# A correlation gram in two half-width blocks of 64 tokens, placed beside attention, in a two-layer f32 kernel

## The chip, the cores and the metric

The kernel runs on one core of a Trainium2 chip. The metric is device microseconds of one execution; of several runs the median counts. The profile is one further execution, recorded by the hardware profiler.

## What is computed

Eight images of 768 channels and 32 x 32 pixels (1024 tokens) pass two layers, each a residual around a group norm.

```python
# layer 0: attention whose scores come from variances
qkv = gn(x).reshape(8, 768, 1024).swapaxes(1, 2) @ W_qkv.T       # 12 heads of 64
scores = var(v) @ var(k).T * scale                               # outer product of two vectors
x = x + proj(softmax(scores) @ v)
# layer 1: 1x1 convolution over 768 channels and 28 correlation channels
f = gn(x)
n = f / max(norm(f over channels), 1e-12)
corr[r, c] = sum over channels of n shifted by (r - 3, c - 3), times n      # zero outside the image
x = x + conv_w @ concat(f, corr at 28 offsets of a 7 x 7 window) + conv_b
```

The 28 offsets are the two diagonals, the middle column and the middle row of the 7 x 7 window. Because a product of two tokens is the same seen from either, the kernel needs only the offsets that look ahead: 12 of them, at most 3 rows down and 3 columns to either side, and the token's product with itself for the norm. The other half is the same numbers shifted.

## The kernel before

Everything is f32. Products of keys and values, of the projection and of the convolution go through a seven-product scheme on blocks (`PAIR`, `SINGLE`, `ORDER`), with `L355` issuing nearly all of them: 128 x 384 moving columns for keys and values, 128 x 512 for projection and convolution. Attention computes, per pair of heads, exponentials on ScalarE (`ex`, L709), and multiplies them with the values on TensorE (`av`, L734): 64 columns for each of two heads, side by side in the array's columns. A run of attention is `STEPS` = 4 key tiles. For some pairs ScalarE also sums the denominators (`junk`, L719), for others VectorE adds the exponentials (`acc`) and TensorE sums them over partitions (`den`). `spread` takes variances on VectorE (`hdk`, `hdv`, `vm`), and `to_rows` transposes them on TensorE (`ptv`, `ptk`, L526) and sends them to DRAM, from where `Pair.rows` broadcasts them (`bc`, `bk`).

Images overlap: while attention of image b runs, the second half of its keys and values and layer 1 of image b - 1 are laid between the runs. The order of all engines' instructions is written by a planner at build time. A `Clock` counts planned microseconds; `later.after` puts a job at a planned time; `work_off` (L1229) takes attention runs whenever they can go, and otherwise the next unit of the list `rest`. Keys-and-values units are planned at `KV_US` = 1.94 us, convolution units at `T_US` = 2.6 us. If only `TAIL` = 14 us of `rest` are left, it waits for attention. Each engine then works strictly in this order. All DMAs but a few at the start go through SP's queue.

The correlation of an image (`Corr`) works on 8 blocks of 128 tokens, 4 rows of the image each. `gram` (L1046) multiplies a block's 128 tokens with the 227 tokens that start with it (`WIN` = 128 + 99), in 6 products over the channels: 128 columns of weights, 227 columns streamed. The last block has 128. The result is copied from PSUM by VectorE (`win`) and written to DRAM (`windowed`, L1056). `diagonals` (L1068) reads from there, with a row pitch one longer than the row, the 19 numbers of each token. `scale` makes the norms (`m`, `rn` on POOL at L1081, `dn`) with a `mask` for the left and right border, transposes (`ct`, L1092) and writes rows; `gather` shifts them and makes the channels `cs`, which the convolution's last products add (L976). The grams are units of 2.35 planned us inside `rest`, in the eighth image one after another behind the first two convolution units.

PSUM tiles of grams and transposes come from `other`, two buffers. POOL makes the sums for keys and values (`make_sums`, L572 to L578). `Conv.start` loads the residual x1 again (`x<-x1d`, L1144) into the buffer of the image whose keys and values are done; VectorE's first take of the convolution needs it. `Norm.apply` writes `f` on VectorE in six pieces.

Of the kernel before, what the change touches and what calls it, by code (L numbers as in the profile page):

```python
# [6 lines left out]
F32 = mybir.dt.float32  # L7
# [20 lines left out]
RUNS = ((0, 0, 4), (31, -1, 3), (62, -2, 5), (93, -3, 7))  # L28
AHEAD_OF = [o for first, _, count in RUNS for o in range(first, first + count)][1:]
NA = len(AHEAD_OF)  # L30
PAD = 99
WIN = P + PAD
# [16 lines left out]
KV_US, T_US, CORR_US = 1.94, 2.6, 1.05  # L49

# [102 lines left out]
def two_layers(ctx, tc, x, wkv, wproj, bproj, wconv, wcorr, bconv, out):  # L153
# [11 lines left out]
    winpool = pool("winpool", 2)  # L165
# [6 lines left out]
    junkpool = pool("junkpool", 1)  # L172
# [230 lines left out]
    windowed = [dconst.tile([MT, P, WIN], F32, name=f"windowed{i}") for i in range(2)]  # L403

    def mask_rows():
        nc.gpsimd.memset(mask, 1.0)
        for q in range(0, P, W):
            at = 0
            for _, right, count in RUNS:
                run = mask[q : q + W, at : at + count]  # L410
                for base, sign in ((right, 1), (W - 1 - right, -1)):
                    nc.gpsimd.affine_select(
                        out=run, in_=run, compare_op=ALU.is_ge, fill=0.0, base=base,
                        pattern=[[sign, count]], channel_multiplier=sign,
                    )
                at += count
# [262 lines left out]
    class Pair:  # L679
# [33 lines left out]
        def denominators(self, t, e):  # L713
# [4 lines left out]
            junk = junkpool.tile([P, N], mybir.dt.bfloat16, tag="junk", name=f"junk{self.b}_{self.hp}_{e}_{t}")  # L718
# [318 lines left out]
    class Corr:  # L1037
        def __init__(self, b, f):
            self.b, self.f = b, f

        def gram(self, t):
            b, f = self.b, self.f
            n = min(WIN, N - t * P)
            ps = other([P, WIN], f"gr{b}_{t}")
            for j in range(J):
                nc.tensor.matmul(  # L1046
                    ps[:, :n], lhsT=f[:, j, t * P : (t + 1) * P], rhs=f[:, j, t * P : t * P + n],
                    start=j == 0, stop=j == J - 1,
                )

            def out():
                win = winpool.tile([P, WIN], F32, tag="win", name=f"win{b}_{t}")
                if n < WIN:
                    vector.memset(win[:, n:WIN], 0.0)
                vector.tensor_copy(win[:, :n], ps[:, :n])
                nc.sync.dma_start(out=windowed[b % 2][t], in_=win)  # L1056
                if t % 4 == 3:
                    later.after(4.0, lambda: self.diagonals(t // 4))

            later.after(2.6, out)  # L1060

        def diagonals(self, hf):
# [4 lines left out]
            for first, _, count in RUNS:  # L1067
                nc.sync.dma_start(  # L1068
                    out=dd[:, :, at : at + count],
                    in_=windows(windowed[b % 2][4 * hf, 0:1, first:], (WIN + 1, P), (P * WIN, 4), (1, count)),  # L1070
                )
                at += count
            later.after(6.0, lambda: self.scale(hf, dd))

        def scale(self, hf, dd):
# [14 lines left out]
            def to_dram(dn):  # L1090
# [3 lines left out]
                vector.tensor_copy(cr, pt[0 : 4 * NROW, 0:P])  # L1094
# [134 lines left out]
    def work_off(rest, attention=None):  # L1229
        while rest or (attention and not attention.over()):  # L1230
            if attention and not attention.over():
                clock.feed_act()
                if attention.can_run():
                    attention.run()
                    continue
# [116 lines left out]
    second = []  # L1352
# [5 lines left out]
    for b in range(NB + 1):  # L1358
        rest, attention, ots = [], None, None
# [5 lines left out]
        if b:  # L1365
# [4 lines left out]
            corr = Corr(b - 1, f)  # L1370
# [3 lines left out]
            grams = [(2.35 if t < MT - 1 else 1.45, has_f, lambda t=t: corr.gram(t)) for t in range(MT)]  # L1374
            first, start = (0.0, has_f, conv.sums.first), (0.0, (), conv.start)
            if b < NB:
                for n, gram in enumerate(grams):
                    rest.insert(2 * (n + 1) + n if b > 1 else 10 + 2 * n, gram)
# [13 lines left out]
        work_off(rest, attention)  # L1392
        if b < NB:
# [4 lines left out]
            elif b + 1 < NB:  # L1398
                clock.wait(("xn", b + 1), ready=ready)
                kv = KeysValues(b + 1, images[b + 1])  # L1400
                work_off(kv.units(0))
# [38 lines left out]
```

## Time and profile before

| | |
|---|---|
| Median of 3 runs | 2721.05 us (2720.9 to 2723.45) |
| Span of the profiled execution | 2722.5 us |
| Its distance from the median | 1.45 us above |
| Granted TensorE clock, mean | 0.998 |
| POOL, `make_sums` (L572 to L578) | 256 operations of 128 x 384, 1.0 to 1.08 us mean |
| VectorE, copy of a gram (`win`) | 64, 0.39 us |
| SP, window writes to DRAM | 64 of 113.5 KB, 0.32 us to issue |
| DMA, all | 448.9 MB, 165 GB/s |

The span is the time from the core's first instruction to its last. A row of a group of instructions gives line, engine, operation, tiles and shape, then how many, the time in which at least one of them ran, the mean length of one, and the idle time of the engine ahead of them. An f32 product appears as two instructions, each with a weight load of its own. [...] what a matmul costs the stream is the distance from its start to the next start.

### The profile page before, as it was taken

To read this page: it belongs to the slowest core of one execution; us is meant where nothing else is said; L and a number is where in the kernel's file an instruction comes from. 1 tells how busy PE (TensorE), PEld (TensorE's weight loads), DVE (VectorE), ACT (ScalarE), POOL (GpSimd) and SP (SyncE) were. 2 spreads that over 40 slices of the span, in tenths; PEclk is the share of its full clock that TensorE was granted. 3 is DMA by queue.
4 is the path that set the end of the run, shared out by engine and by line. 5 is a ranking of instruction groups with operands and counts; after the bars stand their busy time and mean duration, and the time that the engine had idled before them with its cause. 6 is when DMAs were issued, how large, how long until landed. Compare 5 with 4: busy or idle time off the path is not lost.

```text
span 2722.5 us, 28868 instructions
## 1 busy us (share of the span) xinstructions
PE 2685.7 (99%) x9063; PEld 1272.9 (47%) x9063; DVE 1666.8 (61%) x4168; ACT 1362.4 (50%) x1825; POOL 308.0 (11%) x350
## 2 busy tenths in 40 slices
PE   7999999999999999999999999999999999999999
PEld 4443454345543455434654346543465334653354
DVE  5859735785357853588535874357743577436863
ACT  1397078610797008960188601895019850198500
POOL 4320100003100031001210012100121001210000
PEclk9999999999999999999999999999999999999999
DMA  7864455464553655636556365463654526545233
GB/s 275 297 230 137 142 194 146 147 205 147 161 179 112 210 157 160 189 97 206 166 156 185 89 212 174 142 187 92 230 171 137 179 85 233 180 120 162 88 115 101
DMA packets 323603, 448.90 MB, mean 165 GB/s; under 512 B 59714, under 2 KB 245426, under 8 KB 323450
## 3 DMA queue, kind: packets, MB, share of 16 engines
q1 hardware_dynamic: 322218, 444.29, 51.7%
q10 hardware_dynamic: 1232, 2.75, 0.3%
q8 instruction: 73, 1.20, 0.2%
q14 instruction: 80, 0.66, 0.1%
HBM read 377.49 MB, written 67.38 MB: 163 GB/s over the span
## 4 chain that ended last, share of the span: by engine, by line
PE 87%; issue 6%; DVE 4%; DMA 2%; POOL 0%; SPq 0%; ACT 0%; DVEq 0%; POOLq 0%; ACTq 0%
PE x L355 33%; PE av L734 21%; PE y L355 17%; PE z L355 9%; PE gr L1046 3%; DMA x<-x1d 1%; PE den L767 1%; DVE dn L147 1%; PE x L976 1%; PE den L817 1%; DVE t2f L147 1%; PE y L976 1%; PE z L976 1%; DVE cs L147 0%; DMA ws<-in_wkv_dram 0%
## 5 line engine op out<-in xcount | busy, mean ns | idle before, releaser
L709 ACT ACTIVATE ex<-bc,nk 128x1024 f32<-128x1024 f32 x768 | 828.6, 1137 | 501.2 <-DMA bc<-vdr 309.3
L734 PE MATMUL av<-ex,v 128*64 128x512 f32 x3072 | 691.9, 597 | 0.9 <-ACT ex L709 0.8
L719 ACT ACTIVATE junk<-bk,vm 128x1024 bf16<-128x1024 f32 x368 | 420.4, 1142 | 20.0 <-DMA bk<-kdr 13.9
L734 PEld LDWEIGHTS av<-ex,v 128*64 128x64 f32 x3072 | 217.5, 137 | 445.5 <-issue 401.5
L147 DVE TENSOR_TENSOR acc<-acc,ex 128x1024 f32<-128x1024 f32 x350 | 401.9, 1216 | 0.0
L210 ACT COPY kp<-x 128x384 f32<-128x384 f32 x28 | 13.4, 478 | 557.0 <-PE x L355 557.0
L355 PE MATMUL x<-kv,xn 128*128 128x384 f32 x756 | 261.6, 493 | 2.8 <-DMA ws<-in_wkv_dram 1.6
L355 PE MATMUL y<-kv,s 128*128 128x384 f32 x744 | 258.8, 488 | 0.0
L355 PE MATMUL x<-kv,s 128*128 128x384 f32 x744 | 254.3, 488 | 0.0
L355 PEld LDWEIGHTS x<-kv,xn 128*128 128x128 f32 x756 | 142.8, 192 | 113.2 <-issue 17.1
L355 PEld LDWEIGHTS x<-kv,s 128*128 128x128 f32 x744 | 139.3, 190 | 103.4 <-issue 14.1
L355 PEld LDWEIGHTS y<-kv,s 128*128 128x128 f32 x744 | 138.2, 190 | 92.8 <-issue 5.6
L1046 PE MATMUL gr<-f 128*128 128x227 f32 (+1 forms) x672 | 131.4, 345 | 0.0
L355 PE MATMUL x<-v,wt 128*128 128x512 f32 x288 | 130.2, 596 | 0.0
L1046 PEld LDWEIGHTS gr<-f 128*128 128x128 f32 x672 | 121.6, 190 | 16.5 <-issue 3.0
L355 PE MATMUL z<-kv,xn 128*128 128x384 f32 x372 | 126.2, 487 | 0.0
L147 DVE TENSOR_TENSOR v<-y,v 128x128 f32<-128x128 f32 x180 | 41.0, 283 | 122.9 <-PE y L355 122.8
L355 PE MATMUL x<-f,wt 128*128 128x512 f32 x252 | 115.3, 598 | 0.0
L468 POOL TENSOR_TENSOR rstda<-vea,neghalf 128x1 f32<-128x1 f32 x8 | 4.8, 595 | 913.7 <-DVE vea L147 913.7
L147 DVE BATCH_NORM_STATS2 vbn<-v 128x6 f32<-128x64 f32 x720 | 101.9, 213 | 0.0
L572 POOL TENSOR_TENSOR s<-xn 128x384 f32<-128x384 f32 x64 | 68.5, 1080 | 291.7 <-PE x L355 204.7
L355 PEld LDWEIGHTS z<-kv,xn 128*128 128x128 f32 x372 | 70.0, 190 | 48.9 <-issue 3.8
(188 smaller groups left out, 2921.4 us busy)
## 6 DMA issues: line engine op xcount, KB each, us to landing
kv<-kvs SPq DMA_DIRECT2D x124, 576.0 KB
kv<-in_wkv_dram SPq DMA_DIRECT2D x95, 576.0 KB
bc<-vdr SPq DMA_DIRECT2D x96, 512.0 KB
f<-in_x_dram SPq DMA_DIRECT2D x48, 512.0 KB
bk<-kdr SPq DMA_DIRECT2D x46, 512.0 KB
x1d<-f SPq DMA_DIRECT2D x42, 512.0 KB
x<-x1d SPq DMA_DIRECT2D x42, 512.0 KB
out_dram<-x SPq DMA_DIRECT2D x82, 256.0 KB
```

What stands on the lines that cost most here:

```text
L147: return getattr(self.engine, name)(*args, **kw)
L210: nc.scalar.copy(to, at)
L355: nc.tensor.matmul(t, lhsT=lhsT, rhs=rhs, start=p in FIRST and k == 0, stop=stop and k == len(pairs) - 1, skip_group_check=True,)
L468: nc.gpsimd.tensor_tensor(self.rstd, ve, neghalf[:, 0:1], ALU.pow)
L572: nc.gpsimd.tensor_tensor(self.sums[g][:, 0], a[g][2], a[g][3], ALU.add)
L709: nc.scalar.activation(ex, self.bc[e], AF.Exp, scale=self.kv.nk[self.half][:, h, t : t + 1])
L719: nc.scalar.activation(junk, self.bk[e], AF.Exp, scale=self.kv.m2[self.half][:, h, t : t + 1], accum_out=self.sums[:, e, t : t + 1],)
L734: nc.tensor.matmul(self.av[e * HD : (e + 1) * HD, hf, :], lhsT=self.vt[:, t, e, :], rhs=exs[e][:, hf * HF : (hf + 1) * HF], start=t == 0, ...
L767: nc.tensor.matmul(den[at * 32 : (at + 1) * 32, :], lhsT=ones[:, 0:32], rhs=self.acc[e][:, hf * HF : (hf + 1) * HF], start=True, stop=True,)
L817: nc.tensor.matmul(den[e * HD : (e + 1) * HD, :], lhsT=ones, rhs=self.acc[e][:, at], start=True, stop=True)
L976: nc.tensor.matmul(t, lhsT=wcorr_sb[at, i, :], rhs=cs[at, tokens, :], start=False, stop=True, skip_group_check=True)
L1046: nc.tensor.matmul(ps[:, :n], lhsT=f[:, j, t * P : (t + 1) * P], rhs=f[:, j, t * P : t * P + n], start=j == 0, stop=j == J - 1,)
```

## The change

The gram of a block of 4 rows x 32 columns is computed as two blocks of 4 rows x 16 columns (64 tokens), one in each half of the array's columns. Each half streams its own moving operand: 7 rows of the image (`TALL`) by 19 columns (`WIDE`, 16 and 3 more), 133 columns in 7 pieces; 4 rows, 76 columns, for the last block. A weights operand in contiguous order is made first: `turn` copies the block, half by half, with POOL, into one buffer (`turnpool`); for the last image with ScalarE into the buffers of the exponentials, two blocks ahead. The window in DRAM gets another pitch, so that the diagonal read stays one step a token, and is written by two DMAs a gram of 4 x 16 rows of 136 numbers. `mask` follows the new order of tokens and is made of fewer POOL operations and eight small DMAs; the transposed rows are put back in image order by the copy `cr`.

The grams leave `rest` and stand in a list `beside`: `work_off` takes one ahead of and one behind each attention run, with two more given places among the first keys-and-values units from the third loop on (`next_to`), and the remainder ahead of the last units (`remaining`). Each is planned at `GRAM_US` = 1.45 us. `start_corr` makes an image's first turned block during the keys and values of the next image. The scratch output of the denominators shares a buffer with `ds` (`denpool`).

```diff
--- before.py
+++ after.py
@@ -26,10 +26,14 @@
 
 STEP = (33, 32, 31, 1)
 RUNS = ((0, 0, 4), (31, -1, 3), (62, -2, 5), (93, -3, 7))
+HW = W // 2
+TALL, WIDE = MT // 2 + 3, HW + 3
 AHEAD_OF = [o for first, _, count in RUNS for o in range(first, first + count)][1:]
 NA = len(AHEAD_OF)
 PAD = 99
-WIN = P + PAD
+SPAN = TALL * WIDE
+WIN = SPAN + 3
+PITCH = WIN + 3
 ROW = PAD + N + PAD
 NCORR = 28
 NCH = 2 * NA + 4
@@ -47,6 +51,7 @@
 TAIL = 14.0
 EXP, SUM, STEP_US = 1.07, 1.15, 1.77
 KV_US, T_US, CORR_US = 1.94, 2.6, 1.05
+GRAM_US = 1.45
 
 
 
@@ -162,14 +167,13 @@
     vopool = pool("vopool", HP)
     rdpool = pool("rdpool", 1)
     denpool = pool("denpool", 1)
-    winpool = pool("winpool", 2)
     kvpool = pool("kvpool", KVBLOCKS)
     wtpool = pool("wtpool", TBLOCKS)
     sumpool = pool("sumpool", 3)
     bcpool = pool("bcpool", 4)
     bkpool = pool("bkpool", 2)
     expool = pool("expool", 2 * AHEAD)
-    junkpool = pool("junkpool", 1)
+    turnpool = pool("turnpool", 1)
     wk = pool("wk", 3)
     uvpool = pool("uvpool", 1)
     st = pool("st", 1)
@@ -400,20 +404,28 @@
 
 
     rows = [dconst.tile([NROW, ROW], F32, name=f"rows{i}") for i in range(2)]
-    windowed = [dconst.tile([MT, P, WIN], F32, name=f"windowed{i}") for i in range(2)]
+    windowed = [dconst.tile([MT, P * (PITCH + 2)], F32, name=f"windowed{i}") for i in range(2)]
+    wins = [const.tile([P, WIN], F32, name=f"win{i}") for i in range(3)]
+    for win in wins:
+        nc.gpsimd.memset(win, 0.0)
+    across = const.tile([W, NA], F32, name="across")
 
     def mask_rows():
         nc.gpsimd.memset(mask, 1.0)
-        for q in range(0, P, W):
-            at = 0
-            for _, right, count in RUNS:
-                run = mask[q : q + W, at : at + count]
-                for base, sign in ((right, 1), (W - 1 - right, -1)):
-                    nc.gpsimd.affine_select(
-                        out=run, in_=run, compare_op=ALU.is_ge, fill=0.0, base=base,
-                        pattern=[[sign, count]], channel_multiplier=sign,
-                    )
-                at += count
+        nc.gpsimd.memset(across, 1.0)
+        at = 0
+        for _, right, count in RUNS:
+            run = across[:, at : at + count] if at else across[:, 0 : count - 1]
+            right, count = (right, count) if at else (1, count - 1)
+            for base, sign in ((right, 1), (W - 1 - right, -1)):
+                nc.gpsimd.affine_select(
+                    out=run, in_=run, compare_op=ALU.is_ge, fill=0.0, base=base,
+                    pattern=[[sign, count]], channel_multiplier=sign,
+                )
+            at += count
+        for q in range(P // HW):
+            side = q // (P // W)
+            nc.sync.dma_start(out=mask[q * HW : (q + 1) * HW, 1:], in_=across[side * HW : (side + 1) * HW, :])
 
     def load_corr_weights():
 
@@ -715,7 +727,7 @@
             if t == 0 and e == 0:
                 self.sums = st.tile([P, 2, MT], F32, tag="sums", bufs=2, name=f"sums{self.b}_{self.hp}")
             h = self.heads()[e][1]
-            junk = junkpool.tile([P, N], mybir.dt.bfloat16, tag="junk", name=f"junk{self.b}_{self.hp}_{e}_{t}")
+            junk = denpool.tile([P, N], mybir.dt.bfloat16, tag="den", name=f"junk{self.b}_{self.hp}_{e}_{t}")
             nc.scalar.activation(
                 junk, self.bk[e], AF.Exp, scale=self.kv.m2[self.half][:, h, t : t + 1],
                 accum_out=self.sums[:, e, t : t + 1],
@@ -1036,38 +1048,70 @@
 
     class Corr:
         def __init__(self, b, f):
-            self.b, self.f = b, f
+            self.b, self.f, self.turned = b, f, {}
+
+        def turn(self, t):
+
+            last = self.b == NB - 1
+            pl, tag = (expool, "ex") if last else (turnpool, "turn")
+            flat = pl.tile([P, N if last else J * P], F32, tag=tag, name=f"turn{self.b}_{t}")[:, : J * P]
+            self.turned[t] = flat.rearrange("p (j s m) -> p j s m", j=J, s=2)
+            to = flat.rearrange("p (j s y x) -> p j s y x", j=J, s=2, x=HW)
+            rows = self.f[:, :, t * P : (t + 1) * P].rearrange("p j (y s x) -> p j y s x", y=4, s=2)
+            for side in range(2):
+                if last:
+                    act_copy(0.5, to[:, :, side], rows[:, :, :, side, :])
+                else:
+                    nc.gpsimd.tensor_copy(to[:, :, side], rows[:, :, :, side, :])
 
         def gram(self, t):
-            b, f = self.b, self.f
-            n = min(WIN, N - t * P)
-            ps = other([P, WIN], f"gr{b}_{t}")
+
+            b = self.b
+            tall = min(TALL, H - 4 * t)
+            n = tall * WIDE
+            if t not in self.turned:
+                self.turn(t)
+            block = self.turned[t]
+            ps = other([P, SPAN], f"gr{b}_{t}")
             for j in range(J):
-                nc.tensor.matmul(
-                    ps[:, :n], lhsT=f[:, j, t * P : (t + 1) * P], rhs=f[:, j, t * P : t * P + n],
-                    start=j == 0, stop=j == J - 1,
-                )
+                image = self.f[:, j, :].rearrange("p (y x) -> p y x", x=W)
+                for side in range(2):
+                    left = side * (HW - 3)
+                    nc.tensor.matmul(
+                        ps[side * HD : (side + 1) * HD, :n].rearrange("p (y x) -> p y x", x=WIDE),
+                        lhsT=block[:, j, side, :],
+                        rhs=image[:, 4 * t : 4 * t + tall, left : left + WIDE],
+                        start=j == 0, stop=j == J - 1,
+                    )
+            for ahead in range(t + 1, min(t + (3 if b == NB - 1 else 2), MT)):
+                if ahead not in self.turned:
+                    self.turn(ahead)
 
             def out():
-                win = winpool.tile([P, WIN], F32, tag="win", name=f"win{b}_{t}")
-                if n < WIN:
-                    vector.memset(win[:, n:WIN], 0.0)
+                win = wins[t % 2 if t < MT - 1 else 2]
                 vector.tensor_copy(win[:, :n], ps[:, :n])
-                nc.sync.dma_start(out=windowed[b % 2][t], in_=win)
+                for side in range(2):
+                    to = windowed[b % 2][t : t + 1, side * (HD * PITCH + HD - 3) :]
+                    nc.sync.dma_start(
+                        out=windows(to, (HW * PITCH - 3, 4), (PITCH, HW), (1, WIN)), in_=win[side * HD : (side + 1) * HD, :]
+                    )
                 if t % 4 == 3:
                     later.after(4.0, lambda: self.diagonals(t // 4))
 
-            later.after(2.6, out)
+            later.after(GRAM_US + 0.25, out)
 
         def diagonals(self, hf):
 
             b = self.b
             dd = st.tile([P, 4, NA + 1], F32, tag="dd", bufs=2, name=f"dd{b}_{hf}")
             at = 0
-            for first, _, count in RUNS:
+            for down, (_, right, count) in enumerate(RUNS):
                 nc.sync.dma_start(
                     out=dd[:, :, at : at + count],
-                    in_=windows(windowed[b % 2][4 * hf, 0:1, first:], (WIN + 1, P), (P * WIN, 4), (1, count)),
+                    in_=windows(
+                        windowed[b % 2][4 * hf : 4 * hf + 1, down * WIDE + right :],
+                        (PITCH + 1, P), (P * (PITCH + 2), 4), (1, count),
+                    ),
                 )
                 at += count
             later.after(6.0, lambda: self.scale(hf, dd))
@@ -1091,7 +1135,10 @@
                 pt = small(f"ct{b}_{hf}")
                 nc.tensor.transpose(pt[0 : 4 * NROW, 0:P], dn.rearrange("p q r -> p (q r)"), ident)
                 cr = work([4 * NROW, P], f"cr{b}_{hf}")
-                vector.tensor_copy(cr, pt[0 : 4 * NROW, 0:P])
+                vector.tensor_copy(
+                    cr.rearrange("k (y s x) -> k y s x", y=4, s=2),
+                    pt[0 : 4 * NROW, 0:P].rearrange("k (s y x) -> k y s x", s=2, y=4),
+                )
                 for q in range(4):
                     at = PAD + hf * HF + q * P
                     nc.sync.dma_start(out=rows[b % 2][:, at : at + P], in_=cr[q * NROW : (q + 1) * NROW, :])
@@ -1226,12 +1273,25 @@
 
     x1_dram = {}
 
-    def work_off(rest, attention=None):
+    def remaining(beside):
+        while beside:
+            next_to(beside)
+
+    def next_to(beside):
+
+        if beside and ready.issuperset(beside[0][1]):
+            us, _, unit = beside.pop(0)
+            unit()
+            clock.pass_time(us)
+
+    def work_off(rest, attention=None, beside=()):
         while rest or (attention and not attention.over()):
             if attention and not attention.over():
                 clock.feed_act()
                 if attention.can_run():
+                    next_to(beside)
                     attention.run()
+                    next_to(beside)
                     continue
                 if ("v", attention.b, 1) in ready and sum(r[0] for r in rest) <= TAIL:
                     clock.pass_time(0.5)
@@ -1349,14 +1409,18 @@
         for n in range(count):
             later.after(1.0 * n, t_stream.fill)
 
-    second = []
+    def start_corr(b):
+        corrs.append(Corr(b, layer1[b][0]))
+        corrs[-1].turn(0)
+
+    second, corrs = [], []
     later.after(26.0, lambda: sum_weights(1, 9.0, 1.5))
     later.after(50.0, lambda: sum_weights("p", 14.0))
     later.after(82.0, load_second)
     kv, kv1 = KeysValues(0, xn), KeysValues(1, None)
     work_off(kv.units(0))
     for b in range(NB + 1):
-        rest, attention, ots = [], None, None
+        rest, attention, ots, beside = [], None, None, []
         if b < NB:
 
             ots = [v.rearrange("p t r d -> p (t r d)") for v in kv.vt]
@@ -1367,15 +1431,17 @@
             if b > 1:
                 clock.wait(*has_f, ready=ready)
             f, acc = layer1[b - 1] if b > 1 else first_f * 2
-            corr = Corr(b - 1, f)
+            corr = corrs[-1] if 1 < b < NB else Corr(b - 1, f)
             conv = Conv(
                 b - 1, f, None if b < NB else acc, (lambda b=b: next_image(b + 1)) if b + 1 < NB else lambda: None
             )
-            grams = [(2.35 if t < MT - 1 else 1.45, has_f, lambda t=t: corr.gram(t)) for t in range(MT)]
+            grams = [(GRAM_US if t < MT - 1 else 0.9, has_f, lambda t=t: corr.gram(t)) for t in range(MT)]
             first, start = (0.0, has_f, conv.sums.first), (0.0, (), conv.start)
             if b < NB:
-                for n, gram in enumerate(grams):
-                    rest.insert(2 * (n + 1) + n if b > 1 else 10 + 2 * n, gram)
+                beside = grams
+                for n in (3, 7) if b > 1 else ():
+                    rest.insert(n, (0.0, has_f, lambda: next_to(beside)))
+                rest.insert(len(rest) - 4, (0.0, has_f, lambda: remaining(beside)))
                 rest.insert(len(rest) - 4, first)
                 rest += [start] + conv.units()
                 if b == NB - 1:
@@ -1389,7 +1455,8 @@
             more = [(us, (("xn", 1),), unit) for us, _, unit in kv1.units(0)]
             rest += [(0.0, (), apply_second)] + more[:20] + [(0.0, (), lambda: fill_t(3))] + more[20:]
             rest += [(0.0, (), lambda: fill_t(TBLOCKS - 3))]
-        work_off(rest, attention)
+        work_off(rest, attention, beside)
+        assert not beside
         if b < NB:
             project(b, ots, conv.wide if b == NB - 1 else None)
             if b == 0:
@@ -1398,7 +1465,9 @@
             elif b + 1 < NB:
                 clock.wait(("xn", b + 1), ready=ready)
                 kv = KeysValues(b + 1, images[b + 1])
-                work_off(kv.units(0))
+                units = kv.units(0)
+                units.insert(len(units) - 6, (0.0, (("f", b),), lambda: start_corr(b)))
+                work_off(units)
             else:
                 clock.wait(("f", b), ready=ready)
     clock.settle()
```

## The prediction

> **What bounds the kernel now.** I read the page's busy times and the chain of waits first, then the groups of instructions with shapes kept apart, then the timeline of TensorE around the grams, then who waited for whom.
>
> ```profile
> PE 2685.7 (99%) x9063; PEld 1272.9 (47%) x9063; DVE 1666.8 (61%) x4168; ACT 1362.4 (50%) x1825; POOL 308.0 (11%) x350
> ...
> PE 87%; issue 6%; DVE 4%; DMA 2%; POOL 0%; SPq 0%; ACT 0%; DVEq 0%; POOLq 0%; ACTq 0%
> ```
>
> TensorE is busy 2685.7 of 2722.5 us and is 87% of the chain: a microsecond taken from its stream is a microsecond of the span unless it waits for something instead. So I count the stream and then look for new waits.
>
> ```profile
> L734 PE MATMUL av<-ex,v 128*64 128x512 f32 x3072 | 691.9, 597 | 0.9 <-ACT ex L709 0.8
> ...
> L1046 PE MATMUL gr<-f 128*128 128x227 f32 x588 | 120.9, 355 | 0.0
> ...
> L1046 PE MATMUL gr<-f 128*128 128x128 f32 x84 | 10.5, 275 | 0.0
> ```
>
> Columns: instructions, busy us and mean ns, idle before. An f32 product is two instructions in the trace, so one gram (6 products) is 12. The attention products (`av`) load 64 columns; 3072 of them fill 691.9 us, 225 ns each, although one alone needs about 429: they run two at a time, with a different moving operand each. The new gram uses this form.
>
> ```profile
> 1030.59 2.46 PE L1046 MATMUL gr<-f 128*128 128x227 f32 x12
> 1032.89 2.10 PE L355 MATMUL y<-kv,s 128*128 128x384 f32 x6
> 1034.92 7.09 PE L734 MATMUL av<-ex,v 128*64 128x512 f32 x32
> 1041.94 2.20 PE L355 MATMUL x<-kv,s 128*128 128x384 f32 x6
> 1043.98 2.27 PE L1046 MATMUL gr<-f 128*128 128x227 f32 x11
> ```
>
> Start and length in us. Start to start, the gram takes 2.30 us, 192 ns an instruction. An attention run is 16 pairs at 429 ns. Both fit 0.833 ns a column plus 2.5 ns. From 1032.89 to 1043.98 there are 11.09 us; the streams are 6 x 322.5 ns, 16 x 429 ns and 6 x 322.5 ns, 10.74 us. The other 0.35 us is the way from full-width to 64-column products and back.
>
> ```profile
> 1127.96 5.37 PE L734 MATMUL av<-ex,v 128*64 128x512 f32 x24
> 1134.27 0.29 PE L526 MATMUL ptv<-ident,vm 128*48 128x128 f32 x1 [0.93 <-DVE vm L147]
> ...
> 1130.00 0.75 DVE L147 SCALAR_TENSOR_TENSOR x<-x,bconv_sb,x 128x512 f32<-128x512 f32 x1 [4.19 <-PE av L734]
> ...
> 1133.97 0.24 DVE L147 SCALAR_TENSOR_TENSOR vm<-hdv,hsv 128x48 f32<-128x48 f32 x1
> ...
> PE ptv L526 <- DVE vm L147: 8.8, 6, 1.9
> ```
>
> Six times the transpose `ptv`, put inside an attention run, finds `vm` unmade. VectorE was stuck on the convolution's first take at 1130.00: its product ended near 1125, and what came last by the chain of waits is the load of x1 (4.52 us of `x<-x1d` from 1125.39). `vm` stood behind it in the queue.
>
> [...] The stage table shows clock 0.50 from 1470.8 to 1474.2 and from 2143.2 to 2146.6, right after the two longest `ptv` waits. [...] the new moving operand is 7 runs of 19 numbers, and no product before reads in pieces, so the trace can't say. [...]
>
> **The change, part by part**, against the span of 2722.5 us (the median of the runs, 2721.05, is 1.45 lower).
>
> *The grams.* A full one becomes 12 passes of 133 columns on two halves: 133 x 0.833 + 2.5 = 113 ns, 1.36 us for 2.30. The last of an image goes from 128 columns (1.34 us) to 76 (66 ns, 0.79). An image saves 7 x 0.94 + 0.55 = 7.13, eight images 57.0 us. Weights don't bind: 64-column loads of the two halves start 7 ns apart and the next follow 55 ns later, under 66. Unknown is the read in pieces: at best free, at worst the halves share one path and a pass is 226 ns. I take 113, because two different operands already stream at once for `av`.
>
> *The switches.* In the built program's order, images 0 to 6 have grams 2 to 7 (all, in image 0) against an attention run or a neighbour gram: free. In images 1 to 6 grams 0 and 1 stand alone among keys-values products, and the last image's eight stand together: 13 round trips, 4.6 us, less about one that other moves save: +4.2.
>
> *`ptv`.* The six later attention phases now run a whole attention run after the last keys-values product, then `ptv`, then the first convolution units. In VectorE's queue `vm` now stands before the take that waits for x1. After the last keys-values product VectorE has a `kp` sum, six statistics and ten small operations left, about 3.5 us; the run covers 7.0. So 8.8 us of waits go, and with them two half-speed windows that cost 1.7 us each: -12.2 (0 if `vm` is late anyhow). What is late next is the x1 load, now issued after `vdr` and two `bc` loads; its taker is needed only after another attention run and four convolution units (about 25 us after the last product, against an estimated 17).
>
> *The turned blocks.* Two POOL copies of 384 numbers each: [...] the 1.08 us of the two-input L572 rows being the upper side[...]. One buffer, so block t+1 starts when gram t ends. The smallest cover is image 0, one keys-values unit (1.93 us) between grams 1 and 2; everywhere else 5.8 us or more. +0.3. Behind these copies wait `make_sums` and `rn`: in the order, the copy ahead of each waits for a gram that is already past; `ct` keeps about 0.6 us. Nothing for both.
>
> *Image 0's first gram.* It now stands before the attention run that began at 360.00, not after it:
>
> ```profile
> 361.15 0.81 DVE L147 TENSOR_SCALAR f<-f,meanb,rstdb 128x1024 f32<-128x1024 f32 x1 [5.95 <-DMA x1d<-f]
> ```
>
> `f` is whole at 361.96, the two copies end at about 363, and everything on TensorE queues behind: 3 us, and likely a half-speed window: +4.5.
>
> *The end of attention.* With 7 us less to lay beside it, the last two runs of images 2 to 6 now follow each other without the convolution unit between, as in image 7 of before; image 7 itself gets what image 0 has there, two doubled runs with only the sum `den` between.
>
> ```profile
> 2548.64 14.94 PE L734 MATMUL av<-ex,v 128*64 128x512 f32 x64
> ...
> 252.00 3.06 PE L767 MATMUL den<-acc,ones 128*32 128x512 f32 x8 [2.50 <-DVE acc L147]
> ```
>
> A doubled run streams 32 x 0.429 + 0.22 = 13.96 us and takes 14.94, of which gaps between its products show some 0.6 as waits: 5 x 0.6 = +3. For image 7 the 2.5 us wait plus slow clock and gaps: +5.
>
> *The last image.* Gram t+2 needs PSUM freed by VectorE's copy of gram t, behind `t` and `t4f` sums of 2 us each, and every copy but the first two waits for a DMA two grams back. 8 grams stream 10.3 us; I count 12.4 with waits against 0.8 us waited before: +1.3. ACT's copies there (0.48 us in the `kp` rows) stay ahead. More queue entries on SP (a second window write a gram at 0.32 us) lie beside TensorE. Unseen small waits: +2.
>
> Sum: -57.0 + 4.2 - 12.2 + 0.3 + 4.5 + 8 + 1.3 + 2 = -48.9. Span 2673.6, median near 2672; I write 2673.
>
> **Rivals.** (A) *No new waits*: the last four terms vanish, 2721 - 65 = 2656. For: no wait of attention on ACT above 0.8 us now. Against: VectorE's sums at 1.22 us, two a step, are slower than the 1.72 us step. (B) *Attention takes it back*: exponentials (two a step, 2.27 us) can't keep up with runs that come sooner; seven phases lose 3.5 us more each: 2697. For: ACT is busy 54.3 of 56 us from 1072 to 1128. Against: after 1147 it idles 3 to 5 us before each group. (C) *The halves don't overlap for this operand*: a pass of 226 ns makes a gram 2.72 us, +25.6 instead of -57.0: 2755, slower. The change breaks even at a pass of 113 + 49000/768 = 177 ns. Against: the `av` pairs. (D) *The blocks are late*: [...] not a case of its own.
>
> **How the numbers follow.** Mine 0.60, A 0.16, B 0.18, C 0.06. A measurement here can tell 0.2%, 5.4 us. A, B and mine are faster; a little of B and C falls near no change: faster 0.92, same 0.03, slower 0.05. Range: down to A with a little more, up to just past B: 2652 to 2700. The pass length and the `ptv` term make most of it: 10 ns a pass are 7.7 us.
>
> **What would show it.** `gr` at about 57 ns of busy time an instruction, 82 us in all; no wait of `ptv` for `vm`; clock 1.00 where it was 0.50 near 1471 and 2143; a wait of image 0's first gram for a POOL copy; short gaps in doubled runs. Wrong would be a pass well over 113 ns, or TensorE idle before `av` on ACT by tens of microseconds.

## The result, and the profile after

The changed kernel takes 2723.62 us (median of 12 runs, 2720.59 to 2727.77), beside 2721.81 us of the kernel before in the same comparison: a ratio of 1.0011, 95% interval 1.0003 to 1.0020. The forecast was 2673 us, so about 50 us of expected gain are missing. The profiled execution has a span of 2721.6 us, 0.9 us under that of before.

The page of the changed kernel, span and busy times:

```profile
span 2721.6 us, 30651 instructions
...
PE 2649.8 (97%) x9831; PEld 1230.9 (45%) x9831; DVE 1632.4 (60%) x4160; ACT 1365.4 (50%) x1841; POOL 355.3 (13%) x442
```

TensorE is busy for 35.9 us less than before (2685.7), in a span as long as before. The work was taken out and idle time came in. The groups of TensorE with shapes apart show the new gram (columns: busy us and mean ns, then idle ahead):

```profile
L1080 PE MATMUL gr<-f,turn 128*64 128x133 f32 x1176 | 78.5, 282 | 2.9 <-POOL turn L1065 2.9
...
L1080 PE MATMUL gr<-f,turn 128*64 128x76 f32 x168 | 6.7, 229 | 0.0
```

There are twice the instructions, and with the last image's rows (10.4 and 1.0 us) 97 us of busy time where the four rows of before add up to 149.4. The two halves run side by side: the 24 instructions of a gram are 1.53 us of the chain below, 64 ns each, where one of 133 columns alone would take an estimated 113 ns by the fit of the prediction. POOL's groups have the copies at 514 ns each:

```profile
L1065 POOL COPY turn<-f 128x384 f32<-128x384 f32 x112 | 54.5, 514 | 305.4 <-PE gr L1080 292.2 <-DVE f L152 13.2
L1125 POOL TENSOR_TENSOR rn<-m,neghalf 128x4 f32<-128x4 f32 x16 | 16.5, 1032 | 191.7 <-DVE m L152 146.2 <-issue 45.5
```

In the second row, POOL stood for 45.5 us ahead of `rn` with nothing to wait for ("issue"). Where this lands shows in TensorE's list of waits (us in all, times, longest):

```profile
PE ct L1136 <- DVE dn L152: 33.4, 6, 6.2
PE pma L465 <- DVE mva L152: 14.1, 1, 14.1
PE av L746 <- ACT ex L721: 4.6, 4, 2.2
PE den L779 <- DVE acc L152: 3.8, 2, 2.5
```

`ptv`, 8.8 us before, is off the list. In its place six waits of the transpose `ct`, 0.6 us before, take 33.4 us. `pma` was there before; the copies (`turn`) hold a gram up once, for 2.9 us, and takes of VectorE cost 1.8 us. One of the six, by the chain of waits of the changed kernel between 1046 and 1072 us (start, length, what):

```profile
1054.88 1.53 PE gr L1080 x24
...
1056.53 0.96 POOL turn L1065 x2
...
1057.51 0.01 POOLq L1125
...
1057.54 0.01 POOLq L1125
1057.55 7.22 issue
1064.77 1.06 POOL rn L1125
...
1066.81 0.41 PE ct L1136
```

The gram ends, POOL turns the next block, then two control instructions of 11 ns belong to `rn`'s line (their records are named MODIFY_POOL_CONFIG), and 7.22 us pass before `rn` starts. Its input `m` had been there since 1057.06, so `rn` wasn't waiting for data. VectorE (`dn`) and TensorE (`ct`, inside an attention run) stand behind it. The stages of the changed kernel around this wait (stretch, its length, then busy time and count of TensorE, its weight loads, VectorE, ScalarE and POOL, then granted clock, DMA share, GB/s):

```profile
1060.60:1066.80 6.20, 0.94 (x6) 0.08 (x3) 0.80 (x5) 4.06 (x6) 1.05 (x1) 0.98 0.46 157
1066.80:1070.20 3.40, 3.39 (x9) 1.10 (x11) 0.29 (x1) 0.00 (x0) 0.00 (x0) 0.54 0.07 21
```

TensorE idles for 5.27 us of the first stretch and then works for 3.4 us at a clock of 0.54. So this wait costs more than its own length.

Why then, and not in the kernel before? The order of POOL's instructions tells. In the kernel before, the control instructions of `rn` stood directly behind the partition reduction that makes `most` (their records start at 1017.40 and 1017.44), about 38 us ahead of `rn`, and nothing was between. If the 7 us go with them, there were 38 us for it, in which POOL waited for `m` anyhow. POOL's timeline of the kernel before (start, length; in brackets the idle time ahead):

```profile
1017.01 0.44 POOL L649 PARTITION_ALL_REDUCE most<-top  x1 [7.43 <-DVE top L147]
1055.78 1.06 POOL L1081 TENSOR_TENSOR rn<-m,neghalf 128x4 f32<-128x4 f32 x1 [38.33 <-DVE m L147]
```

In the changed kernel the copies of `turn` 1 to 5 stand between, each waiting for a gram, and the control instructions come behind the last of them. POOL's timeline of the changed kernel:

```profile
1018.84 0.43 POOL L661 PARTITION_ALL_REDUCE most<-top  x1 [7.43 <-DVE top L152]
1023.65 0.96 POOL L1065 COPY turn<-f 128x384 f32<-128x384 f32 x2 [4.38 <-PE gr L1080]
...
1064.77 1.05 POOL L1125 TENSOR_TENSOR rn<-m,neghalf 128x4 f32<-128x4 f32 x1 [7.28 <-issue]
```

The first copy starts when its gram is done, 4.38 us behind the reduction. So a COPY runs behind the reduction without the 7 us, and a TENSOR_TENSOR seems to need them. This is theory R, the author's reading of these rows: after a partition reduction POOL has to be prepared for a TENSOR_TENSOR, which takes 7 us, and the preparation starts only when its place in the queue is reached. What the 7 us consist of the trace doesn't show: between the copy's end and `rn` POOL has the two control records alone, and the list of DMA packets from 1057.4 to 1064.8 those of q1, the kernel's own queue. There are two rivals: theory C, the chain `win`, `windowed`, `dd`, `m` is late or POOL waits for something else; theory B, attention takes back what the grams leave, which was a rival of the prediction.

### The profile page after: what moved, and what is told of

Read it like the earlier page. It is cut to its first block, busy times and chain, and to the rows that moved or that the text cites. A ratio compares the mean times of both kernels' runs of the same rounds, so it can differ in the third digit from the quotient of the medians.

```text
span 2721.6 us, 30651 instructions
## 1 busy us (share of the span) xinstructions
PE 2649.8 (97%) x9831; PEld 1230.9 (45%) x9831; DVE 1632.4 (60%) x4160; ACT 1365.4 (50%) x1841; POOL 355.3 (13%) x442
## 4 chain that ended last, share of the span: by engine, by line
PE 89%; DMA 5%; issue 3%; DVE 2%; ACT 1%; POOL 1%; SPq 0%; DVEq 0%; POOLq 0%; ACTq 0%
PE x L359 35%; PE av L746 22%; PE y L359 17%; PE z L359 9%; PE gr L1080 3%; DMA x<-x1d 1%; DMA di<-ir 1%; PE den L779 1%; DMA rd<-di 1%; PE x L988 1%; PE den L829 1%; PE y L988 1%; DMA vdr<-rsv 1%; PE z L988 1%; ACT ex L721 0%
## 5 line engine op out<-in xcount | busy, mean ns | idle before, releaser
L746 PE MATMUL av<-ex,v 128*64 128x512 f32 x3072 | 705.3, 604 | 4.8 <-ACT ex L721 4.6
L746 PEld LDWEIGHTS av<-ex,v 128*64 128x64 f32 x3072 | 230.5, 138 | 442.7 <-issue 380.1
L152 DVE COPY win<-gr 128x133 f32<-128x133 f32 x64 | 18.4, 288 | 128.2 <-PE gr L1080 118.6
L1065 POOL COPY turn<-f 128x384 f32<-128x384 f32 x112 | 54.5, 514 | 305.4 <-PE gr L1080 292.2
L152 DVE SCALAR_TENSOR_TENSOR x<-x,bconv_sb,x 128x512 f32<-128x512 f32 x63 | 45.8, 746 | 78.1 <-DMA x<-x1d 55.9
```

The source lines that it names most:

```text
L152: return getattr(self.engine, name)(*args, **kw)
L746: nc.tensor.matmul(self.av[e * HD : (e + 1) * HD, hf, :], lhsT=self.vt[:, t, e, :], rhs=exs[e][:, hf * HF : (hf + 1) * HF], start=t == 0, ...
L1065: nc.gpsimd.tensor_copy(to[:, :, side], rows[:, :, :, side, :])
```

## The experiments

**e1: the preparation moved forward.** A tiny TENSOR_TENSOR behind the reduction; TensorE's order stays as in the changed kernel, instruction for instruction.

```diff
             nc.gpsimd.partition_all_reduce(most, top, P, bass_isa.ReduceOp.max)
+            early = st.tile([P, 4], F32, tag="early", name=f"early{name}")
+            nc.gpsimd.tensor_tensor(early, neghalf, neghalf, ALU.mult)
```

> One tiny POOL TENSOR_TENSOR stands directly behind the partition reduction that makes `most`; TensorE's order and all the rest are as in the changed kernel. Theory R (POOL has to be made ready again after the partition reduction before it can run a TENSOR_TENSOR, 7.2 us, and the turned copies kept that from happening early): rn follows m within 0.2 us, the six `ct` waits of 33.4 us go to under 2 us, the six half-clock windows (about 1.7 us each) go too, and the time falls by 33.4 + 10 = about 43 us, to 2675 to 2685. Theory C (the chain win, windowed, dd, m is what is late, or POOL's idle 7.2 us is a wait for something else): rn stays 7 us behind m, time 2720 to 2726. Theory B (attention takes back whatever grams leave): the `ct` waits go, waits on exponentials come in their place, time 2712 to 2724.

Measured: 2677.72 us (4 runs), ratio to the kernel before 0.9837, interval 0.9822 to 0.9851. POOL's timeline of e1:

```profile
1016.88 0.19 POOL L663 TENSOR_TENSOR early<-neghalf 128x4 f32<-128x4 f32 x1 [7.22 <-issue]
...
1046.92 0.96 POOL L1067 COPY turn<-f 128x384 f32<-128x384 f32 x2 [8.49 <-PE gr L1082]
1047.84 1.06 POOL L1127 TENSOR_TENSOR rn<-m,neghalf 128x4 f32<-128x4 f32 x1
```

The 7.22 us stand behind the reduction now, beside other work, and `rn` follows the copy at once. `ct` is off TensorE's waits. The span is 2675.5 us, 46.1 under the changed kernel's: 33.4 us are the waits. Within and behind the six waits the granted clock was 0.50 for 3.4 or 6.8 us each; TensorE worked for 22 us of that time, so an estimate of what half speed cost is 11 us. The remaining 1.7 us lie elsewhere: e1 has one other stretch of slow clock (at 479 us), where the changed kernel has three (at 251, 473 and 483 us). Rivals C and B fall.

**e10: the control.** The same place, the same numbers, but a COPY.

```diff
+            nc.gpsimd.tensor_copy(early, neghalf)
```

> The control to e1: at the same place behind the partition reduction a POOL COPY of the same 128x4 numbers instead of a TENSOR_TENSOR. Theory R, with what it says of kinds (a COPY runs without the preparation, a TENSOR_TENSOR needs it): rn stays 7 us behind m and the six `ct` waits stay, 2720 to 2727, as the changed kernel's 2723.6. Rival: any instruction behind the reduction makes POOL ready, 2675 to 2680 as with the TENSOR_TENSOR.

Measured: 2723.94 us (20 runs), ratio 1.0011, interval 1.0005 to 1.0018, as the changed kernel. POOL's timeline of e10:

```profile
1018.49 0.44 POOL L661 PARTITION_ALL_REDUCE most<-top  x1 [7.42 <-DVE top L152]
1018.82 0.25 POOL L663 COPY early<-neghalf 128x4 f32<-128x4 f32 x1
...
1064.03 1.05 POOL L1127 TENSOR_TENSOR rn<-m,neghalf 128x4 f32<-128x4 f32 x1 [6.89 <-issue]
```

The COPY started 0.33 us after the start of the reduction and prepared nothing: `rn` still came after 6.89 us of "issue". Of the two kinds tried, only the TENSOR_TENSOR brought the preparation with it (7.22 us ahead of `early` in e1).

**e3: the loss made in the kernel before.** One copy of 4 numbers a partition ahead of `rn`, with the grams of old.

```diff
+            mc = st.tile([P, 4], F32, tag="mc", name=f"mc{b}_{hf}")
+            nc.gpsimd.tensor_copy(mc, m)
-            nc.gpsimd.tensor_tensor(rn, m, neghalf, ALU.pow)
+            nc.gpsimd.tensor_tensor(rn, mc, neghalf, ALU.pow)
```

> The kernel before, with one POOL copy of m (128x4) ahead of rn, nothing else: TensorE's order is that of the kernel before. Theory R: making POOL ready can start only behind this copy, so rn comes 7 us after m in six images, `dn` and the evictions queued behind it on VectorE are late by that, and the old kernel loses 5 to 7 us plus a half-clock window six times: 2755 to 2775. Theory C or B: a copy of about 0.1 us changes nothing, 2719 to 2724.

Measured: 2787.32 us, ratio 1.0236, interval 1.0219 to 1.0254. POOL's timeline of e3 and then its wait on TensorE:

```profile
1066.43 0.19 POOL L1082 COPY mc<-m 128x4 f32<-128x4 f32 x1 [38.24 <-DVE m L147]
1076.43 1.05 POOL L1083 TENSOR_TENSOR rn<-mc,neghalf 128x4 f32<-128x4 f32 x1 [9.82 <-issue]
```

```profile
PE ct L1094 <- DVE dn L147: 55.6, 6, 9.9
```

A copy of 0.19 us, made 16 times, costs 65 us: 55 us more of `ct` waits and slow clock behind them. In direction theory R holds here without any of the change; in size it was too low. The preparation took 8.6 to 9.8 us in these six places (7.2 to 8.2 in the changed kernel), and `ct` had almost no slack to spend. Why it is longer here wasn't tried.

**e2: `ct` moved instead.** `rn` stays late, `ct` leaves the attention run.

```diff
-                later.after_dve(0.7 if b else 4.0, lambda: to_dram(dn))
+                later.after_dve(8.7 if b and b < NB - 1 and hf == 0 else 0.7 if b else 4.0, lambda: to_dram(dn))
```

> The transpose `ct` of each first half is handed out 8 us later, which puts it behind nine more matmuls of keys and values instead of into an attention run; the turned copies and rn stay as in the changed kernel. Theory R: rn is still 7.2 us late, but `ct` no longer stands in front of TensorE's work when it is; ct waits under 3 us, time 2675 to 2690, the upper end if VectorE's evictions, which stand behind `dn`, now hold TensorE up instead. Theory C: the same if the chain is late for another reason, so this run tells only that the place of `ct` is what turns lateness into time. Theory B: 2712 to 2724.

Measured: 2673.66 us, ratio 0.9822, interval 0.9808 to 0.9837. `rn` starts after 6.96 us of "issue" at 1054.26, and TensorE meets `ct` at 1060.26 without a wait. So a late `rn` costs time only through the place of `ct`. The time is 4 us under that of e1. TensorE's order has six round trips between 128 and 64 columns less than in e1 (0.35 us each, 2.1 us), as `ct` no longer stands inside an attention run; the rest is within what such runs tell, since e6 next, with TensorE's order of e2, took 1.8 us more.

**e6: both.** The edits of e1 and e2 together.

> Both cures at once: the early TENSOR_TENSOR behind the partition reduction, and `ct` of the first halves 8 us later. Theory R: each alone removes the same loss, so together they bring little more than the later `ct` alone (2673.7): the four evictions of about 1 us in all behind the late rn go, 2669 to 2674. Rival: there are two separate losses, which add up: 2650 or less.

Measured: 2675.48 us, ratio 0.9831, interval 0.9816 to 0.9846: within 2 us of e2, though 1.5 us above the range of theory R. Far from 2650: it is one loss, not two.

**e9: the grams twice.** On top of e6, to price the term that the forecast rests on.

```diff
-            for j in range(J):
+            for turn, j in enumerate([*range(J), *range(J)]):
...
-                        start=j == 0, stop=j == J - 1,
+                        start=turn == 0, stop=turn == 2 * J - 1,
```

> As e6, with each product of a gram added twice (the norms come from the same grams, so the factor cancels). Theory: the grams lie wholly on TensorE's path, so a second set of 1.36 us a gram (0.79 the last of an image), 8 images, costs 8 x (7 x 1.36 + 0.79) = 82 us over e6: 2750 to 2760, and the halving of the gram really gave the 57 us of the prediction. Rival: beside attention part of a gram fills time in which TensorE would wait, so the second set costs clearly less, 30 to 65 us.

Measured: 2756.37 us, 80.9 above e6 (82.9 by the spans, 2754.1 and 2671.2), where 82 was worked out. The profiled run of e9 has two stretches of slow clock in image 1, of 3.4 us each, that e6 lacks, an estimated 3.4 us of the 82.9. So a set of new grams costs about its full length on TensorE, 80 to 83 us, and the length is the one predicted.

**e5: the grams at their old places.** With e1's TENSOR_TENSOR.

```diff
-                beside = grams
-                for n in (3, 7) if b > 1 else ():
-                    rest.insert(n, (0.0, has_f, lambda: next_to(beside)))
-                rest.insert(len(rest) - 4, (0.0, has_f, lambda: remaining(beside)))
+                for n, gram in enumerate(grams):
+                    rest.insert(2 * (n + 1) + n if b > 1 else 10 + 2 * n, gram)
```

> The early TENSOR_TENSOR, but the grams stand where the kernel before had them, among the keys-values products, in the new form of two halves. Theory: what placing beside attention runs is worth is the switches between 128 and 64 columns, 46 more of them in TensorE's order than in the changed kernel, at 0.175 us each = 8 us; 2681 to 2690 beside 2677.7 with the early TENSOR_TENSOR alone. Rival 1: the placement also did away with the `ptv` waits of the kernel before (8.8 us and two half-clock windows), and they return here: 2690 to 2700. Rival 2: the placement is worth nothing or costs attention time, under 2678.

Measured: 2687.74 us, ratio 0.9875, interval 0.9859 to 0.9892, 10.0 above e1. Of TensorE's waits in e5:

```profile
PE gr L1082 <- POOL turn L1067: 11.0, 6, 2.4
```

46 more switches are 8.0 us by the estimate; grams wait 8.1 us longer for their copies (2.9 in e1), which was not expected; `av` waits 3.5 less for exponentials (1.3 for 4.8). These three make 12.6, against 12.4 between the spans (2687.9 and 2675.5); smaller terms are left out. Placing beside attention is worth these 10 to 12 us. The `ptv` waits don't return, so placing the grams beside attention isn't needed to remove them.

**e4, e8, e11, e12: image 1.** The other new loss of the changed kernel lies at 471 to 486 us, in the seventh attention run of image 1. Its chain of waits there, in the changed kernel:

```profile
456.90 0.19 DVE rsv L152
...
457.12 9.06 DMA vdr<-rsv
...
466.57 4.86 DMA bc<-vdr
```

`rsv` goes to DRAM and comes back as row copies `bc`, 14 us, and the exponentials are late. Four edits, of which e4 builds on e1, e8 on e6, e11 on e2 and e12 on e11:

```diff
 # e4: the planner counts on the rows 6 us later
-(6.0 if self.hp % (HP // 2) else 9.0 if self.hp else first)
+(6.0 if self.hp % (HP // 2) else (15.0 if self.b == 1 else 9.0) if self.hp else first)
 # e8: the convolution's first loads earlier in image 1
-                rest += [start] + conv.units()
+                rest.insert(len(rest) - (3 if b == 1 else 0), start)
+                rest += conv.units()
 # e11: ScalarE takes rsv
+        if name == "v1_1":
+            act_copy(0.3, rs, pt[0 : MT * HH, 0:P])
 # e12: and three x1 loads 9 us later
+                    us += 9.0 * (self.b == 0 and n in (1, 3, 4))
```

> The early TENSOR_TENSOR of e1, and in image 1 the planner is told that the second half's row copies land 6 us later (15 instead of 9), so it puts other work ahead of the seventh attention run. Theory: the 4.6 us of `ex` waits there and two half-clock windows, 7.6 us together, are not inherent; 2667 to 2677, 7 us under e1. Rival: the exponentials of that run are late whatever stands ahead, and the wait comes back one run later or at the image's end: same time as e1 within 2 us.

> As e6, and in image 1 the convolution's first loads are issued three products earlier, so that VectorE, which waits 5 us for `x<-x1d` ahead of the copy `rsv`, should be free sooner and the row copies of the second half land sooner. Theory: the 4.6 us of `ex` waits of image 1's seventh and eighth attention steps go with their half-clock time, 5 to 8 us under e6. Rival: `rsv` now stands behind the wait for `rd` instead and comes no sooner: within 2 us of e6.

> As e2 (later `ct`), and in image 1 alone the copy `rsv` of the second half is taken by ScalarE instead of VectorE. Theory: `rsv` is late because it stands in VectorE's queue behind a take that waits for `x<-x1d` (and behind `v<-v,rd` where that take was moved); on ScalarE it follows `ptv` at once, the row copies `bc` land some 5 us sooner, and the waits of image 1's seventh attention run on `ex` (5.5 us, with slow clock up to 7.5) go: 2666 to 2670 beside 2673.7. Rival: the two transfers `vdr<-rsv` and `bc<-vdr`, 14 us together, are what is late, and start no sooner because the sync queue stands on loads of its own: 2672 to 2676.

> As e11 (ScalarE takes `rsv` in image 1), and the three x1 loads of 512 KB that stood in the sync queue ahead of `vdr<-rsv` there are issued 9 us later, behind the row copies `bc`. Theory: `vdr<-rsv` took 9.97 us because it lies behind 1.5 MB of x1 and a weight block in the same queues; at some 350 GB/s the three are 4.4 us, and with 2 us less on the sync queue `bc` lands about 5 us sooner, at 466; the seventh run's waits on `ex` fall from 5.6 us to under 2, time 2668 to 2672 (e2: 2673.7). Rival: the takes of the convolution, which need those x1 loads, now wait instead, on VectorE and through PSUM on TensorE: 2674 to 2682.

Measured: 2677.35 (e1: 2677.72), 2675.18 (e6: 2675.48), 2677.94 and 2673.28 us (e2: 2673.66). None gains: in e4 and e8 the time is that of the rival, e11 lies above both of its ranges, e12 between its two. In e4, e8 and e12 the wait moves, in e11 it stays (5.6 us of `av` for `ex`). In e4 it is then a transpose (`it`, 2.9 us) and a load (`cs`, 2.4); in e8 `rsv` stands behind `v<-v,rd`, whose load VectorE awaits for 14.18 us, and TensorE waits 5.0 for a take. In e11 ScalarE has `rsv` done at 453.43, but SP issues `vdr` only at 456.18, behind x1 loads, and its transfer takes 9.97 us. The 350 GB/s of the forecast of e12 was near what the changed kernel moved from 471 to 475 us, 360 GB/s. In e12 SP issues `vdr` at 453.39 and `bc` at 460.80, 5.4 us sooner; the waits on `ex` are gone, and TensorE's waits read:

```profile
PE x L359 <- DVE x L152: 6.8, 4, 5.1
```

Now the take waits for the x1 loads that were put off. That VectorE's queue alone makes the seventh run late is refuted by e11. One reading fits all four: the loads of this stretch are late together, and putting one ahead makes another the last. No run takes loads away altogether, so it stays a reading.

## Why the prediction was wrong

The step that failed is in "The turned blocks": "Behind these copies wait `make_sums` and `rn`: in the order, the copy ahead of each waits for a gram that is already past; `ct` keeps about 0.6 us. Nothing for both." The copy is indeed past in time: at 1057.49 it ends 0.4 us after `m`. But the copies also came between the partition reduction and `rn`, and carried the preparation of 7 us, hidden until then, to a place where `m`, `dn` and `ct` stand behind it. The prediction looked for what waits behind the moved instructions and priced each at its busy time. It put this term at nothing without asking what POOL did in the 38 us in which it seemed to do nothing. What the runs showed instead: `rn` starts 7.2 to 8.2 us behind the copies in six images, `ct` makes TensorE wait for 33.4 us in all, and with the slow clock behind these waits the term is about 44 to 46 us (e1). A hint was in the trace of before, in POOL's timeline of its first phase:

```profile
80.31 0.40 POOL L649 PARTITION_ALL_REDUCE most<-top  x1 [10.10 <-issue]
87.65 2.09 POOL L572 TENSOR_TENSOR s<-xn 128x384 f32<-128x384 f32 x1 [6.95 <-PE x L355]
```

There are 10 us of "issue" ahead of the reduction, and 6.95 us between it and the next TENSOR_TENSOR, which the view puts down to TensorE.

Term by term, against the span of before:

| Term | Put at, us | Measured, us |
|---|---|---|
| grams | -57.0 | -56.6: old set 8 x (7 x 2.30 + 1.34) = 139.5, new set 82.9 (e9, spans; 80 by the estimate above) |
| switches | +4.2 | +2.8: 16 changes more in TensorE's order, 0.35 us a pair |
| `ptv` waits, slow clock | -12.2 | -12.2: no wait listed, clock 1.00 at 1461 to 1466 and 2131 to 2136 |
| turned blocks | +0.3 | 0 outside image 0; a copy took 514 ns, a length that no trace of before had shown |
| image 0's first gram | +4.5 | +2.9, no slow clock behind it |
| end of attention | +8 | +4.3: doubled runs 14.94 us as put (+3), `den` 3.8 for 2.5 |
| last image | +1.3 | +0.9: 1.7 us of idle ahead of its grams for 0.8 |
| unseen | +2 | +1.8 takes, +6.6 image 1 |
| `rn`, `ct` | 0 | +46.1 (changed kernel less e1) |

Image 1's term is 4.6 us of waits and, at a clock of 0.70 over 4 us and 0.68 over 5 us, 2.8 us of slow clock, less 0.8 waited before. The right column sums to -3.4; the spans differ by -0.9, so 2.5 us have no name. The last row is a difference of two runs and holds some slow clock at 251 us and in image 1 as well, an estimated 3.5 us, in part counted in the row above too. Without the last row the sum is -49.5, where the prediction had about -49, with errors of both signs in it (the end of attention and image 0 too dear, image 1 not seen). e1 shows that sum on the chip: 2675.5 us of span, 47.0 under before.

The main mechanism, two halves side by side at 113 ns a pass, was right, and rival C (halves in turn, 226 ns) is refuted by e9. The sign named for it, 82 us of busy time, didn't come as worded: busy time is 97 us, as the records of matmuls overlap (in the kernel before, one of 227 columns is 355 ns long and the next starts after 192; 149.4 us of busy time there, for a stream of 139.5). Rival B, attention taking the time back, is refuted by e1, in which `av` waits 4.8 us for exponentials, hardly more than the 4.6 of the changed kernel. Rival A, no new waits, is what none of the runs reached. The reason given for `ptv` was right too: in the changed kernel a whole attention run stands between the last keys-values product and `ptv`, and VectorE makes `vm` long before the first take that waits for x1. `ptv` follows at 1124.77 without a wait:

```profile
1120.84 0.25 DVE L152 SCALAR_TENSOR_TENSOR vm<-hdv,hsv 128x48 f32<-128x48 f32 x1
...
1136.61 0.75 DVE L152 SCALAR_TENSOR_TENSOR x<-x,bconv_sb,x 128x512 f32<-128x512 f32 x1 [8.47 <-DMA x<-x1d]
```

In e5, with other places for the grams, `vm` (at 1106.98) also stands ahead of that take (1116.05). The chance of 0.03 for no change was too small for what the prediction knew of POOL: its rows were read as busy times alone.

## What to carry to other kernels

When instructions are put into an engine's queue, ask what state the engine is in there, and not only what they cost: here a preparation that had been hidden moved with the first instruction that needed it. If a change takes work out and the time stays, compare busy time with the span, then follow the new wait back to the first engine that waited for nothing. A preparation can be drawn forward with one tiny instruction of the right kind, or its consumer can be moved out of the way; both brought the gain back here (2677.72 us in e1, 2673.66 in e2), and the second alone is as good as any version that ran.

## What the runs showed of the hardware

- In e1, e3 and the changed kernel, POOL's first TENSOR_TENSOR behind a PARTITION_ALL_REDUCE began 6.7 to 9.8 us after POOL had ended the instruction ahead of it, wherever nothing else was late, and copies in between didn't shorten that. A COPY came at once (0.33 us from start to start in e10).
- Each of the twelve waits for `ct` in the changed kernel and e3 (5.2 to 9.9 us) had a stretch of clock 0.50 that began within it, of 3.4, 6.8 or 10.2 us. Shorter waits differ: `ptv` waits of 1.83 and 1.94 us in the kernel before and the `den` wait of 2.50 us at 251 us (clock 0.69 over 251 to 256) had one at their end or within 1.3 us behind it, the 2.9 us ahead of image 0's first gram had none.
- A moving operand of 7 pieces of 19 numbers cost no more here than an unbroken one: 1.36 us a gram is 133 columns at the price of before, and e9's 80 to 83 us a set agree with it.
- VectorE's small operations took longer while POOL worked. In e3, where POOL's two-input sums run right behind `rn`, `dn` takes nearly six times as long as in the changed kernel, where POOL is idle then. (In the kernel before it takes 0.98 and 3.93 us too, so this is no part of e3's loss.) VectorE's timelines, e3 first and then the changed kernel:

```profile
1077.52 0.98 DVE L147 COPY dn<-rn 128x4 f32<-128x4 f32 x1 [11.16 <-POOL rn L1083]
1078.41 3.91 DVE L147 SCALAR_TENSOR_TENSOR dn<-dd,rn,mask 128x19 f32<-128x19 f32 x4
```

```profile
1065.86 0.17 DVE L152 COPY dn<-rn 128x4 f32<-128x4 f32 x1 [8.79 <-POOL rn L1125]
1065.98 0.68 DVE L152 SCALAR_TENSOR_TENSOR dn<-dd,rn,mask 128x19 f32<-128x19 f32 x4
```

The factor was 5.8 for both kinds, the COPY (0.98 us for 0.17) and the four SCALAR_TENSOR_TENSORs (3.91 for 0.68). The length goes with that of POOL's instruction rather than by a factor: in both kernels, e1, e2 and e3 together, one such SCALAR_TENSOR_TENSOR took 227 to 242 ns in 240 cases with POOL idle, 545 to 548 ns in 6 cases under POOL's copies of 0.51 us, and 1026 to 1066 ns in 74 cases under its sums of about 1 us. No run changed this alone, so that POOL is the cause is the author's reading, not shown.
